# Bias terms of two mixture-of-experts layers: from fp32 matmuls to bfloat16 matmuls on three-part splits

## The chip, the cores and the metric

The kernel runs on one core of a Trainium2 chip. Its time is the device time of one execution in microseconds (us). The core's engines work in parallel, each through its own instruction stream in a fixed order: TensorE (PE, matmuls), VectorE (DVE), ScalarE (ACT), GpSimd (POOL, which here issues gathers and scatters by index) and SyncE (SP, which issues DMAs). They wait for each other through semaphores.

## What is computed

A network of four layers on 3125 nodes of width 256 (padded to 25 tiles of 128 rows) with 53125 edges. Each layer is a graph part and a dense part, each with a residual. The change concerns the dense parts of layers 2 and 3:

```python
# layer 2: eight experts, all used, weighted by a softmax router
w = softmax(feat @ Wr + br)
h = relu(bn(einsum('bfd,edh->bfeh', x, W1) + b1))
h = relu(bn(einsum('bfeh,ehk->bfek', h, W2) + b2))
y = einsum('bfeh,ehd->bfed', h, Wo) + bo            # bo: 8 x 256
out = einsum('bfed,fe->bfd', y, w)
# layer 3: a shared MLP and four experts, the two best gates per node
shared = relu(relu(x @ sW1 + sb1) @ sW2 + sb2) @ sW3 + sb3     # sb3: 1 x 256
o = einsum(relu(... experts ...), eW3) + eb3                   # eb3: 4 x 256
gates = softmax(x @ gW + gb); topv, topi = top_k(gates, 2)
out = shared + sum(softmax(topv) * o[topi])
```

In both layers the experts' last bias enters the output as (weights of the node) x (bias table): a product with a contraction of 8 or of 4.

## The kernel before

The program is laid out by a scheduler: it takes the operations as the code lists them, and fixes the order on each engine by its own estimates, so that a listed operation can move past others. The work goes through the layers in turn. The edges are worked on in 52 chunks of 8 tiles of 128 edges, the nodes in seven groups (GROUPS): six of four tiles and one of a single tile.

**Layer 2.** The edge loop is in l2_sorted (L1032 to L1089): for each chunk SP loads xw, row and rb (L1017 to L1024), TensorE makes the filters and messages, VectorE multiplies (xs, L1075), and POOL adds the rows into tables in memory (L1089). In its twelfth pair of tiles it calls late_weights, which loads all weights of the dense part: W1, W2, Wo (large), Wr, the router's bias br, bo (plain, one DMA), and two sets of normalisation vectors b, g, be, m, v, which VectorE folds together (L1130 to L1133). Then comes dense_sorted. For each group, choose (L1219 to L1232) makes the router's weights v (128 nodes x 8 per tile), transposes them on TensorE (L1230, one transpose per tile) and copies them to vT (8 x 128 per tile). experts then runs eight experts, two layers of fp32 matmuls into ph (L155) and ScalarE's ReLU to SBUF (L1249), and the last layer po, which VectorE adds with weight v into the residual (L1277). Ahead of the first expert's po, the bias term is one fp32 matmul per tile, vT against bo (L1269), 8 rows contracted, added at L1271. The choice for the next group is listed between the experts of the current one.

**Layer 3.** The edge loop is in l3_sorted: per chunk a load of the destination row (dl, L670), eight gathers of POOL (L208), masks sT (L679), maxima (ao L692, top L700, seg_m L431), products (L736) and a scatter as matmuls (L750). The first time a tile of nodes is met, its rows xh are loaded (L685). At its fifth chunk it calls l3_weights, which loads all weights of the dense part. A bias that is added by a matmul goes through bias3: load, split on VectorE into three bfloat16 parts (L1340, L1342) and a DMA that puts the parts on three rows (L1344); so it is for gb and sb3. eb3 is a plain load. sel is a 4 x 256 fp32 table of ones, made on POOL by blocks (L145 to L148), which spreads an expert's weight to the 64 rows of its hidden units. Then l3_dense: front, turn and choose make the gates of a group, spread transposes them (L852) and copies them to wT (L854), and experts runs the shared MLP and the experts. The expert's hidden values are multiplied by their gates at he (L894), with the gates spread by one fp32 matmul pk of sel and wT per pair of experts (L891, 4 rows contracted, 512 columns). The output po of a tile (L155) sums five matmuls: hs x sW3, ones x sb3 (bfloat16, 3 rows), wT x eb3 (fp32, 4 rows), and two of he x eW3. Each group's choice is listed inside the group before it (hooks 0 to 2).

What the change rewrites:

```python
                    self.mm(po, [(hs[:, c], w_["sW3"][:, 0, :]), (self.ones3, w_["sb3"]),
                                 (wT[:, j, :], w_["eb3"])]
                            + [(he[:, i, c], w_["eW3"][:, i, :]) for i in range(2)])
```

Of the kernel before, what the change touches and what calls it, by code (L numbers as in the profile page):

```python
# [8 lines left out]
F32 = mybir.dt.float32  # L9
BF = mybir.dt.bfloat16  # L10
# [7 lines left out]
P = 128  # L18
# [28 lines left out]
class Net:  # L47
# [93 lines left out]
    def blocks(self, pool, ne, width, name):  # L141

        nc = self.nc
        t = pool.tile([ne, ne * width], F32, name=name)
        nc.gpsimd.memset(t, 1.0)  # L145
        nc.gpsimd.affine_select(t, t, pattern=[[1, ne * width]], base=0, channel_multiplier=-width,
                                compare_op=ALU.is_ge, fill=0.0)
        nc.gpsimd.affine_select(t, t, pattern=[[-1, ne * width]], base=width - 1,  # L148
                                channel_multiplier=width, compare_op=ALU.is_ge, fill=0.0)
        return t  # L150


# [609 lines left out]
    def l3_weights(self, wp):  # L762
        w = {n: self.rows(wp, f"L3_ffn_{n}") for n in ("sW1", "sW2", "sW3", "eW1", "eW2", "eW3",
                                                       "gW")}
        w |= {n: self.plain(wp, f"L3_ffn_{n}") for n in ("sb1", "sb2", "eb1", "eb2")}
        w["gb"] = self.bias3(wp, "L3_ffn_gb")
        w["sb3"] = self.bias3(wp, "L3_ffn_sb3")
        w["eb3"] = self.plain(wp, "L3_ffn_eb3")
        w["sel"] = self.blocks(wp, 4, 64, "sel4")
        w["it"] = self.iota_row(wp, 4)  # L770
        return w

    def l3_dense(self, wp, o, a, b):

        nc, tc = self.nc, self.tc
        NE = 4
        w_ = self.l3w
        NG = len(GROUPS)
        with ExitStack() as ctx:
            work = ctx.enter_context(tc.tile_pool(name="work", bufs=2))  # L780
            psum = ctx.enter_context(tc.tile_pool(name="psum", bufs=2, space=PSUM))
            ab = work.tile([P, 2, D], F32, name="ab", bufs=1)
            for i, v in enumerate((a, b)):
                tp = psum.tile([P, 2, P], F32, name="tp")
# [3 lines left out]
            ys, xTs, ws = {}, {}, {}  # L788
# [57 lines left out]
            def spread(g):  # L846

                t0, n = GROUPS[g]
                oh = ws[g]
                tp = psum.tile([NE, 4, P], F32, name="sm", bufs=1)  # L850
                for j in range(n):
                    nc.tensor.transpose(tp[:, j, :], oh[:, j, :], self.ident)  # L852
                wT = work.tile([NE, 4, P], F32, name="wT")
                nc.scalar.copy(wT[:, :n], tp[:, :n])  # L854
                ws[g] = wT

            def experts(g, hooks):
                t0, n = GROUPS[g]
                w = n * P
                xT, wT = xTs.pop(g), ws.pop(g)  # L860

                def hidden(to, pairs, b):
                    ph = psum.tile([P, 4 * P], F32, name="ph", bufs=3)
                    self.mm(ph[:, :w], pairs)
                    nc.scalar.activation(to[:, :w], ph[:, :w], AF.Relu, bias=b)

                h1 = work.tile([P, 2, 4 * P], F32, name="h1")
                for f in range(2):
                    hidden(h1[:, f, :], [(w_["sW1"][:, k, f * P:(f + 1) * P], xT[:, k, :w])
                                         for k in range(2)], w_["sb1"][:, f:f + 1])  # L870
                hooks.get(0, lambda: None)()
                e1s = []
                for e in range(NE):
                    e1 = work.tile([P, 4 * P], F32, name="e1", bufs=5)
                    hidden(e1, [(w_["eW1"][:, 2 * e + k, :], xT[:, k, :w]) for k in range(2)],
                           w_["eb1"][:, e:e + 1])
                    e1s.append(e1)
                hooks.get(1, lambda: None)()
                hs = work.tile([P, 4 * P], F32, name="hs")
                hidden(hs, [(w_["sW2"][:, k, :], h1[:, k, :w]) for k in range(2)], w_["sb2"])  # L880
                he = work.tile([P, 2, 4 * P], F32, name="he")
                for i in range(2):
                    ph = psum.tile([P, 4 * P], F32, name="ph", bufs=3)
                    for j in range(2):
                        e = 2 * i + j
                        nc.tensor.matmul(ph[64 * j:64 * j + 64, :w], w_["eW2"][:, e, :],  # L886
                                         e1s[e][:, :w], start=True, stop=True)
                    r = work.tile([P, 4 * P], F32, name="r")
                    nc.scalar.activation(r[:, :w], ph[:, :w], AF.Relu, bias=w_["eb2"][:, i:i + 1])
                    pk = psum.tile([P, 4 * P], F32, name="ph", bufs=3)  # L890
                    nc.tensor.matmul(pk[:, :w], w_["sel"][:, i * P:(i + 1) * P],  # L891
                                     wT[:, :n].rearrange("e t p -> e (t p)"), start=True,
                                     stop=True)
                    nc.vector.tensor_mul(he[:, i, :w], r[:, :w], pk[:, :w])  # L894
                hooks.get(2, lambda: None)()
                y = work.tile([P, 4, D], F32, name="yo")
                for j in range(n):
                    t = t0 + j
                    c = slice(j * P, (j + 1) * P)
                    po = psum.tile([P, D], F32, name="po")  # L900
                    self.mm(po, [(hs[:, c], w_["sW3"][:, 0, :]), (self.ones3, w_["sb3"]),
                                 (wT[:, j, :], w_["eb3"])]
                            + [(he[:, i, c], w_["eW3"][:, i, :]) for i in range(2)])
                    nc.vector.tensor_add(y[:, j, :], self.x[:, t, :], po)
                    r = P if t < NT - 1 else LAST
                    nc.sync.dma_start(self.out[t * P:t * P + r, :], y[:r, j, :])
                hooks.get(3, lambda: None)()
# [208 lines left out]
    def late_weights(self, wt, after):  # L1116

        nc = self.nc
        self.after = after
        w1, w2, wo = (self.rows(wt, f"L2_ffn_{n}") for n in ("W1", "W2", "Wo"))  # L1120
        wr = self.rows(wt, "L2_ffn_Wr")
        br = self.bias3(wt, "L2_ffn_br")
        bo = self.plain(wt, "L2_ffn_bo")

        ab = []
        for i in "12":
            b_, g_, be, m_, v_ = (self.plain(wt, f"L2_ffn_{n}{i}")
                                  for n in ("b", "g", "be", "m", "v"))
            r = self.rsqrt(wt, v_, 1e-3, [P, 16], f"bn{i}")
            nc.vector.tensor_mul(r, r, g_)  # L1130
            nc.vector.tensor_sub(b_, b_, m_)
            nc.vector.tensor_mul(b_, b_, r)
            nc.vector.tensor_add(b_, b_, be)  # L1133
            ab.append((r, b_))
        w = self.with_attention(wt, "L3_gnn_W", 8, ("L3_gnn_att_src", "L3_gnn_att_dst"))
        self.after = None
        return w1, w2, wo, wr, br, bo, ab, w

    def dense_sorted(self, tables, wu1, bu1, wu2, bu2, gamma, beta, late):

        nc, tc = self.nc, self.tc
        w1, w2, wo, wr, br, bo, ab, w3 = late
        NE = 8
        with ExitStack() as ctx:
# [66 lines left out]
            def choose(g):  # L1211

                t0, n = GROUPS[g]
                xT = xTs[g] = turned(g, xTs[g])
                pl = psum.tile([P, 4, NE], F32, name="sm", bufs=1)
                for j in range(n):
                    self.mm(pl[:, j, :], [(xT[:, k, j * P:(j + 1) * P], wr[:, k, :])
                                          for k in range(2)] + [(self.ones3, br)])
                v = work.tile([P, 4, NE], F32, name="v")  # L1219
                mx = work.tile([P, 4], F32, name="mx")  # L1220
                mb = mx[:, :n].unsqueeze(2).to_broadcast([P, n, NE])
                nc.vector.tensor_reduce(mx[:, :n], pl[:, :n], axis=AX.X, op=ALU.max)
                nc.vector.tensor_sub(v[:, :n], pl[:, :n], mb)
                nc.scalar.activation(v[:, :n], v[:, :n], AF.Exp)
                nc.vector.tensor_reduce(mx[:, :n], v[:, :n], axis=AX.X, op=ALU.add)
                nc.vector.reciprocal(mx[:, :n], mx[:, :n])
                nc.vector.tensor_mul(v[:, :n], v[:, :n], mb)
                pT = psum.tile([NE, 4, P], F32, name="sm", bufs=1)
                for j in range(n):
                    nc.tensor.transpose(pT[:, j, :], v[:, j, :], self.ident)  # L1230
                vT = work.tile([NE, 4, P], F32, name="vT")
                nc.scalar.copy(vT[:, :n], pT[:, :n])  # L1232
                ws[g] = v, vT

            def experts(g, hooks):
                t0, n = GROUPS[g]
# [1024 lines left out]
```

## Time and profile before

| | us |
|---|---|
| median of 3 runs | 3889.32 |
| lowest and highest of them | 3887.5, 3907.43 |
| the profiled execution | 4120.86 |
| its span, first to last instruction | 4119.1 |
| layer 2: first to last bias matmul (L1269) | 2535.0 to 3086.2 |
| layer 3: first to last matmul with eb3 | 3935.8 to 4112.5 |

The profile is of one execution, with times from the start of its span. An instruction's line begins with its start and duration in us, then the engine, the line of the code, the operation, out<-in, the shape and how many in a row. An fp32 matmul is recorded as two. Matmuls overlap, so their durations add up to more than the time they take; their starts do not. "idle before" in brackets is how long the engine had stood still, and what released it. PEclk is the clock that TensorE was granted, in tenths of full speed in the page, as a fraction in a table of stretches. The tables by stretches give for each engine its busy time in that stretch with the number of instructions in brackets. Names lose their numbers in the trace: L_ffn_bo is layer 2's bo, and L_ffn_eb and L_ffn_sb in the matmuls of po are eb3 and sb3.

### The profile page before, as it was taken

How to read it: one execution, taken by the hardware profiler on the slowest of the kernel's cores; microseconds unless marked ns; L12 is line 12 of the kernel's file. 1: busy time of each engine (PE TensorE's matmuls, PEld its weight loads, DVE VectorE, ACT ScalarE, POOL GpSimd, SP SyncE). 2: the span in 40 equal slices, each digit the busy share in tenths (PEclk: the TensorE clock that was granted, in tenths of full speed). 3: DMA queues.
4: the chain of work that ended last, by engine and by line, in shares of the span. 5: the costliest groups of instructions: out<-in, count | busy, mean ns of one | idle time of the engine just before them, and what ended most of it. 6: DMA issues, size and time to landing. Idle time of an engine off the chain costs nothing. (4 is left out here: it accounts for less than half of the span.)

```text
span 4119.1 us, 46662 instructions
## 1 busy us (share of the span) xinstructions
PE 3364.1 (82%) x15552; PEld 2332.5 (57%) x15552; DVE 2200.9 (53%) x5404; ACT 966.1 (23%) x2102; POOL 1683.2 (41%) x1510
## 2 busy tenths in 40 slices
PE   3598879999996367999999989999992456665699
PEld 2365367777773245777777754556662344544554
DVE  4672379999998237433434333222332455655741
ACT  2222200000001124444444423333331000000142
POOL 4200146666661217777777740000005455654000
PEclk7799989999998679999999999999996677777789
DMA  4631378888882467887777860000004443443000
GB/s 129 201 125 44 134 230 270 284 281 272 272 274 71 146 202 195 165 133 128 134 132 128 134 136 3 6 6 6 6 6 126 113 111 104 117 111 100 21 11 22
DMA packets 339898, 524.03 MB, mean 127 GB/s; under 512 B 64375, under 2 KB 246849, under 8 KB 339649
## 3 DMA queue, kind: packets, MB, share of 16 engines
q0 software_dynamic: 125040, 236.91, 26.9%
q1 hardware_dynamic: 207217, 276.70, 21.3%
q10 hardware_dynamic: 7392, 7.34, 0.5%
q8 instruction: 126, 2.06, 0.2%
q14 instruction: 123, 1.01, 0.1%
HBM read 389.15 MB, written 131.64 MB: 126 GB/s over the span
## 5 line engine op out<-in xcount | busy, mean ns | idle before, releaser
L1089 POOL DMA_INDIRECT t<-sm,to x416 | 659.5, 1585 | 191.4 <-ACT sm L1086 68.4
L208 POOL DMA_INDIRECT kv<-kv_d,src_i x416 | 428.1, 1029 | 616.8 <-DVE s L412 348.3
L208 POOL DMA_INDIRECT xa<-xa_d,src_i x416 | 397.4, 955 | 312.6 <-issue 232.6
L155 PE MATMUL pe<-L_gnn_We,ea 128*128 128x256 f32 x1664 | 442.6, 389 | 28.9 <-issue 11.8
L750 PE MATMUL acc<-xa,s 128*128 128x272 f32 x1312 | 380.1, 445 | 89.1 <-DVE s L741 50.3
L155 PEld LDWEIGHTS <-sT 128*128 128x128 bf16 x3152 | 271.1, 100 | 279.8 <-issue 180.3
L1072 PE MATMUL pf<-L_gnn_Wf,hf 128*128 128x256 f32 x1664 | 419.7, 396 | 7.6 <-ACT hf L1035 7.6
L750 PEld LDWEIGHTS acc<-xa,s 128*128 128x128 f32 x1312 | 278.1, 219 | 166.8 <-DVE s L741 52.4
L1072 PEld LDWEIGHTS pf<-L_gnn_Wf,hf 128*128 128x128 f32 x1664 | 302.6, 192 | 88.9 <-issue 46.9
L1075 DVE TENSOR_TENSOR xs<-xs,pf 128x512 f32<-128x512 f32 x208 | 142.8, 687 | 376.9 <-PE pf L1072 338.3
L155 PEld LDWEIGHTS pe<-L_gnn_We,ea 128*128 128x128 f32 x1664 | 294.5, 194 | 85.2 <-DVE kv L526 31.7
L145 POOL MEMSET sel<- 4x256 f32 x1 | 0.3, 302 | 688.8 <-PE tp L155 688.8
L526 DVE TENSOR_TENSOR kv<-kv,pe 128x1024 f32<-128x1024 f32 x208 | 254.5, 1223 | 23.9 <-remote 19.4
L554 PE MATMUL acc<-kv,s 128*128 128x264 f32 x832 | 225.0, 395 | 11.1 <-DVE kv L549 6.9
L1084 PE MATMUL ps<-xs,m 128*128 128x256 f32 x832 | 217.0, 384 | 20.6 <-DVE xs L1075 16.3
L1249 ACT ACTIVATE h<-ph,L_ffn_b,bn_r 128x512 f32<-128x512 f32 (+1 forms) x224 | 162.8, 732 | 290.3 <-PE ph L155 289.9
L1277 DVE SCALAR_TENSOR_TENSOR xres<-po,v,xres 128x256 f32<-128x256 f32 x200 | 96.2, 482 | 247.7 <-PE po L155 247.4
L1086 ACT COPY sm<-ps 128x512 f32<-128x512 f32 x208 | 121.9, 586 | 451.3 <-PE ps L1084 363.3
L155 PE MATMUL po<-L_ffn_Wo,h 128*128 128x256 f32 x800 | 196.2, 389 | 0.0
L155 PE MATMUL qx<-qw,sT 128*128 128x256 bf16 x1248 | 190.9, 275 | 4.9 <-DVE pr L528 3.7
L155 PE MATMUL ph<-xT,L_ffn_W 128*128 128x512 f32 (+1 forms) x448 | 185.3, 553 | 0.5 <-ACT h L1249 0.5
L1084 PEld LDWEIGHTS ps<-xs,m 128*128 128x128 f32 x832 | 159.3, 192 | 44.5 <-issue 10.6
(434 smaller groups left out, 5424.1 us busy)
## 6 DMA issues: line engine op xcount, KB each, us to landing
ea<-in_edge_attr_dram SPq DMA_DIRECT2D x52, 1024.0 KB
dl<-dlT_d SPq DMA_DIRECT2D x156, 256.0 KB
row<-src_d SPq DMA_DIRECT2D x52, 512.0 KB
xs_d<-zero SPq DMA_DIRECT2D x2, 7168.0 KB
xg<-xs_d SPq DMA_DIRECT2D x28, 512.0 KB
t<-zero SPq DMA_DIRECT2D x4, 3328.0 KB
seg<-seg_d SPq DMA_DIRECT2D x52, 256.0 KB
qw<-q_d SPq DMA_DIRECT2D x52, 192.0 KB
```

The lines of the kernel that those rows point to most:

```text
L155: self.nc.tensor.matmul(out, l, r, start=(i == 0), stop=(i == len(pairs) - 1))
L208: self.nc.gpsimd.indirect_dma_start(out=out, out_offset=None, in_=table, in_offset=bass.IndirectOffsetOnAxis(ap=ids, axis=0))
L526: nc.vector.tensor_add(kvv, kvv, pe[:, :, None, :].to_broadcast([P, 2, 2, D]))
L554: nc.tensor.matmul(acc, s1[:, j, :], kv[:, j, D:], start=((t + j) % EL == 0), stop=((t + j) % EL == EL - 1))
L750: nc.tensor.matmul(accs[T][:, :R + 8], s1[:, i, :], xa[:, j, :], start=begins and i == 0, stop=last[T] == b and j == js[-1])
L1072: nc.tensor.matmul(pf[:, j, :], hf[:, c % 4, k, j * P:(j + 1) * P], wf2[:, k, :], start=False, stop=j + k == 2)
L1075: nc.vector.tensor_mul(xs, xs, pf)
L1084: nc.tensor.matmul(ps[:, j, :], m[:, (2 * c + j) % EL, :], xs[:, j, :], start=True, stop=True)
L1086: nc.scalar.copy(sm, ps)
L1089: nc.gpsimd.indirect_dma_start(out=tables[(2 * c + j) % len(tables)], in_=sm[:, j, :], in_offset=None, compute_op=ALU.add, out_offset=bass ...
L1249: nc.scalar.activation(h[:, f, :w], ph[:, :w], AF.Relu, scale=ab[i][0][:, c:c + 1], bias=ab[i][1][:, c:c + 1])
L1277: nc.vector.scalar_tensor_tensor(xv[:, i, :], po[:, i, :], v[:, j + i, e - 2:e - 1], xv[:, i, :], op0=ALU.mult, op1=ALU.add)
```

## The change

The weights of a node's experts and the bias tables are each split into three bfloat16 parts (value, remainder, remainder of that), and all nine products of parts are summed in one bfloat16 matmul: 9 x 8 = 72 rows in layer 2, 9 x 4 + 3 = 39 in layer 3, whose last three rows are ones against the parts of sb3. New functions, with the calls that use them:

```diff
+    def products(self, pool, names, ones):
+        nc = self.nc
+        k, n = self.ins[names].shape
+        t = pool.tile([9 * k + (3 if ones else 0), n], BF, name=f"{names}_9")
+        def parts(name, k):
+            a = pool.tile([8, n], F32, name="pr_a")[:k]
+            self.held(a)
+            nc.sync.dma_start(a, self.ins[name])
+            p = pool.tile([8, 3, n], BF, name="pr_p")[:k]
+            for i in range(3):
+                nc.vector.tensor_copy(p[:, i, :], a)
+                if i < 2:
+                    nc.vector.tensor_sub(a, a, p[:, i, :])
+            return p
+        p = parts(names, k)
+        for j in range(3):
+            for i in range(3):
+                r = (3 * j + i) * k
+                nc.sync.dma_start(t[r:r + k, :], p[:, j, :])
+        if ones:
+            nc.sync.dma_start(t[9 * k:, :], parts(ones, 1))
+        return t
+    def thirds(self, work, psum, v, n, k, ones):
+        nc = self.nc
+        w = 9 * k + (3 if ones else 0)
+        r = work.tile([P, 4, w], BF, name="w9")
+        if ones:
+            nc.vector.memset(r[:, :n, 9 * k:], 1.0)
+        d = work.tile([P, 4, k], F32, name="w9_d")
+        for i in range(3):
+            part = r[:, :n, i * k:(i + 1) * k]
+            nc.vector.tensor_copy(part, v if i == 0 else d[:, :n])
+            if i < 2:
+                nc.vector.tensor_sub(d[:, :n], v if i == 0 else d[:, :n], part)
+        for j in range(1, 3):
+            nc.vector.tensor_copy(r[:, :n, 3 * j * k:3 * (j + 1) * k], r[:, :n, :3 * k])
+        tp = psum.tile([w, 4, P], F32, name="sm", bufs=1)
+        for j in range(n):
+            nc.tensor.matmul(tp[:, j, :], r[:, j, :], self.identb, start=True, stop=True)
+        t = work.tile([w, 4, P], BF, name="wT")
+        nc.scalar.copy(t[:, :n], tp[:, :n])
         return t
...
-        w["sb3"] = self.bias3(wp, "L3_ffn_sb3")
-        w["eb3"] = self.plain(wp, "L3_ffn_eb3")
-        w["sel"] = self.blocks(wp, 4, 64, "sel4")
+        w["b3"] = self.products(wp, "L3_ffn_eb3", "L3_ffn_sb3")
+        sel = self.blocks(wp, 4, 64, "sel4")
+        b = wp.tile([4, 4 * 64], BF, name="sel4_b")
+        self.nc.vector.tensor_copy(b, sel)
+        w["sel"] = wp.tile([39, 4 * 64], BF, name="sel39")
+        self.nc.vector.memset(w["sel"], 0.0)
+        for i in range(3):
+            self.nc.sync.dma_start(w["sel"][4 * i:4 * i + 4, :], b)
...
-                oh = ws[g]
-                tp = psum.tile([NE, 4, P], F32, name="sm", bufs=1)
-                for j in range(n):
-                    nc.tensor.transpose(tp[:, j, :], oh[:, j, :], self.ident)
-                wT = work.tile([NE, 4, P], F32, name="wT")
-                nc.scalar.copy(wT[:, :n], tp[:, :n])
-                ws[g] = wT
+                ws[g] = self.thirds(work, psum, ws[g], n, NE, True)
...
-                    self.mm(po, [(hs[:, c], w_["sW3"][:, 0, :]), (self.ones3, w_["sb3"]),
-                                 (wT[:, j, :], w_["eb3"])]
+                    self.mm(po, [(hs[:, c], w_["sW3"][:, 0, :]), (wT[:, j, :], w_["b3"])]
...
-        bo = self.plain(wt, "L2_ffn_bo")
+        bo = self.products(wt, "L2_ffn_bo", None)
...
-                pT = psum.tile([NE, 4, P], F32, name="sm", bufs=1)
-                for j in range(n):
-                    nc.tensor.transpose(pT[:, j, :], v[:, j, :], self.ident)
-                vT = work.tile([NE, 4, P], F32, name="vT")
-                nc.scalar.copy(vT[:, :n], pT[:, :n])
-                ws[g] = v, vT
+                ws[g] = v, self.thirds(work, psum, v[:, :n], n, NE, False)
```

The matmuls L891 and L1269 are written as before; their operands are now bfloat16 tiles of 39 and 72 rows. In order of engines: SP issues 21 DMAs more (nine for bo, nine for eb3, three for sel39), and between the loads of late_weights and l3_weights; VectorE gets the splits of the tables (five operations each), a cast and a memset for sel39, and seven (layer 2) or eight (layer 3) small operations per group; ScalarE's copy of the transposed weights writes bfloat16 and more rows.

More of the change, by code (lines that the diff above doesn't have):

```diff
@@ L149, in blocks @@
                                 channel_multiplier=width, compare_op=ALU.is_ge, fill=0.0)
+        return t
[20 more added lines that the diff above has]
+            nc.sync.dma_start(t[9 * k:, :], parts(ones, 1))
+        return t
+    def thirds(self, work, psum, v, n, k, ones):
[17 more added lines that the diff above has]
+        nc.scalar.copy(t[:, :n], tp[:, :n])
         return t
```

## The prediction

> **What bounds the kernel now.** I read the page first (shares, then the 40 slices), then the stretches of the span that the change touches, then the order of time on single engines inside them.
>
> ```profile
> PE 3364.1 (82%) x15552; PEld 2332.5 (57%) x15552; DVE 2200.9 (53%) x5404; ACT 966.1 (23%) x2102; POOL 1683.2 (41%) x1510
> ...
> PE   3598879999996367999999989999992456665699
> ...
> PEclk7799989999998679999999999999996677777789
> ```
>
> TensorE is busiest, but only in some slices. A saved matmul is worth its time only where the PE row shows 9, so I cut the span by stage:
>
> ```profile
> core 0: us, PE busy (x) PEld busy (x) DVE busy (x) ACT busy (x) POOL busy (x), PEclk, DMA share, GB/s
> ...
> 1600.00:1680.00 80.00, 68.42 (x360) 48.70 (x358) 51.23 (x184) 42.09 (x103) 55.70 (x35) 0.94 0.99 235
> 1680.00:2430.00 750.00, 740.85 (x4189) 554.30 (x4188) 291.06 (x1082) 302.19 (x546) 585.32 (x371) 1.00 0.78 127
> ...
> 2600.00:3095.00 495.00, 494.49 (x1734) 299.77 (x1733) 152.72 (x451) 172.12 (x270) 0.00 (x0) 0.99 0.02 6
> 3115.00:3250.00 135.00, 26.87 (x173) 19.77 (x173) 38.05 (x93) 5.54 (x18) 77.54 (x85) 0.55 0.52 145
> 3250.00:3910.00 660.00, 401.63 (x1958) 309.30 (x1957) 381.73 (x853) 51.81 (x193) 321.08 (x336) 0.76 0.35 95
> 3910.00:3930.00 20.00, 12.55 (x61) 9.87 (x61) 17.59 (x68) 12.06 (x27) 0.00 (x0) 0.67 0.00 1
> 3930.00:4119.00 189.00, 183.90 (x646) 96.76 (x646) 55.25 (x240) 57.35 (x99) 0.00 (x0) 0.93 0.05 18
> ```
>
> The fourth row is layer 2's dense experts and the last is layer 3's: TensorE fills 99.9% and 97% of them, VectorE 31% and 29%. There matmul time is kernel time. The rows 1600 to 1680 and 3115 to 3250 are where the weights are loaded. The first is crowded in its DMA (0.99), the second in nothing: layer 3's edge loop waits for latencies.
>
> **What it removes on TensorE.** The durations of single matmuls overlap, so I take start to start:
>
> ```profile
> 2626.57 1.13 PE L1269 MATMUL po<-L_ffn_bo,vT 8*128 8x256 f32 x4
> 2627.63 1.13 PE L155 MATMUL po<-L_ffn_Wo,h 128*128 128x256 f32 x4
> ...
> 4017.68 1.12 PE L891 MATMUL ph<-wT,sel 4*128 4x512 f32 x2
> 4018.73 1.08 PE L886 MATMUL ph<-e,L_ffn_eW 128*64 128x512 f32 x4
> ...
> 4020.79 0.60 PE L852 MATMUL sm<-ident,oh 128*4 128x128 f32 x4
> 4021.22 0.60 PE L155 MATMUL po<-L_ffn_sW,hs 128*128 128x256 f32 x2
> 4021.75 0.28 PE L155 MATMUL po<-L_ffn_sb,ones 3*128 3x256 bf16 x1
> 4021.87 0.59 PE L155 MATMUL po<-L_ffn_eb,wT 4*128 4x256 f32 x2
> 4022.40 0.92 PE L155 MATMUL po<-L_ffn_eW,he 128*128 128x256 f32 x3
> ```
>
> An fp32 matmul shows as two records. L1269: 4 records, two matmuls, 1.06 us, 0.53 each. L891: 1.05. The transposes of L852 (an identity matmul of one record each): 0.43 for four, 0.11 each. The bf16 matmul of sb3, 256 wide: 0.12. The expert bias after it: 0.53.
>
> Layer 2: 25 tiles x (0.53 - 0.12) = 10.3 us. The transposes become bf16 matmuls with 128 columns to stream, half of sb3's; I take half of its 0.12, so they save 25 x 0.05 = 1.3. Together 11.5 us.
>
> Layer 3, each group of four tiles: po loses the separate bias matmul and turns the fp32 one to bf16, (0.12 + 0.53) - 0.12 = 0.53 a tile, 2.1 us; transposes 0.2; L891 twice. For a bf16 matmul 512 wide the nearest row is layer 2's loop:
>
> ```profile
> 1700.94 0.38 PE L1068 MATMUL pf<-L_gnn_bf,ones 3*128 3x512 bf16 x1
> 1701.26 1.99 PE L1072 MATMUL pf<-L_gnn_Wf,hf 128*128 128x256 f32 x8
> ```
>
> That is 0.32 us. [...] So a full group saves 1.46 + 2.1 + 0.2 = 3.8 us, six of them 22.7; the one-tile group about 1.0. Together 23.7 us at full clock, a little more in the profiled execution, whose clock was 0.93 there. That 36 or 39 or 72 rows are contracted instead of 4 or 8 costs nothing by these rows: 3 rows took 0.12, and xe's 128 rows took 0.13 (1700.18 to 1700.94 for six).
>
> **What it adds on VectorE and ScalarE in these stages.** Per group seven small operations in layer 2 and eight in layer 3, about 0.2 us each and 0.21 start to start, so 1.5 to 1.7 us between the weights and their transposes. Layer 2: the weights were ready at 2693.7 (L1227 at 2693.51, 0.19 long), so the parts are at 2695.2, or 2695.7 with one L1277 of 0.48 between. The changed order puts the transposes behind two more ph matmuls, which end near 2696: a stall of 0 to 0.3 us a group, I take 1 us in all. ScalarE's copy stays as large (0.57). Layer 3: choose ends at 4043.6, the transposes come at 4051.2; 7.6 us of cover for 1.7, so nothing. Without that cover it would be 6 x 1.7 = 10 us. Only the first, one-tile group has none: VectorE fills 17.6 of 20 us there, so 8 operations at 0.15 to 0.21 cost about 2 us. The he products wait for L891's result as before, but it comes sooner; VectorE stays far below full, so TensorE remains the bound.
>
> **What it adds in loading.** Layer 2's bias goes through VectorE (five operations of 8x256, 0.3 to 0.4 each, 1.7 us) and nine scattering DMAs, inserted on SP between these and the loop's own loads:
>
> ```profile
> 1640.12 0.33 SPq L129 DMA_DIRECT2D L_ffn_v<-in_L_ffn_v_dram  x1
> 1640.54 0.38 SPq L129 DMA_DIRECT2D L_ffn_b<-in_L_ffn_b_dram  x1
> 1641.01 0.39 SPq L129 DMA_DIRECT2D L_ffn_g<-in_L_ffn_g_dram  x1
> ...
> 1645.28 0.38 SPq L1020 DMA_DIRECT2D xw<-x_d  x1
> ```
>
> SP issues one each 0.45 us: 9 x 0.45 = 4 us, by which m, v, w_att and the next chunks' xw, row and rb move back. PE waited 4.5 us for that xw (at 1650.41) already. From 1680 TensorE is full (741 of 750), so lateness is not made up: +4 us, bounds 0 (gather and scatter waits cover it) and 8 (the nine also wait for the split on VectorE, with xs multiplications, L1075, queued behind). [...]
>
> Layer 3's weights: twelve more DMAs on SP (nine parts, three for sel39; sb3's one takes the place of its old one), and on VectorE five small operations more for eb3, a cast and a memset. SP already hangs here:
>
> ```profile
> 3147.45 0.47 SPq L685 DMA_DIRECT2D xh<-xa_d  x1
> 3176.45 0.76 SPq L1344 DMA_DIRECT2D L_ffn_gb<-L_ffn_gb_p  x1
> ```
>
> It waits 28.5 us for the split of gb, which stands on VectorE behind a 26.12 us wait at L692. Before, dl of two further chunks was issued ahead of this block; in the changed order only one is, and the other comes after nine scatters, gb's, a seg load and the load of sb3, 12 x 0.45 = 5 us after the block lifts. Who waits: sT (L679), then pa, then the ao and top of that chunk; and VectorE's split of sb3 waits for the nine DMAs, since it reuses their tile. Below nothing: earlier order could also help this latency-bound stretch. Bounds -10 to +50; I take +3, since VectorE reaches those chunks only at 3185 to 3188, about when the late load lands. The cast of sel waits for POOL's blocks, done at 3118.5: nothing.
>
> **Sum.** -11.5 + 1 (layer 2), -23.7 + 2 (layer 3), +4 and +3 (loads) = -25 us. In the profiled execution: 4120.86 (span 4119.1) to about 4096. That execution stands 231 us above the median of 3889.32, mostly in layer 3's loop and clock, which the change's gains don't touch; the dense stages ran near full clock, so I carry the 25 us over unscaled: 3864 us, -0.65%. About 0.5%, 19 us, is what this measurement can tell from no change.
>
> **Rivals.**
> 1. Layer 3's loop start gets worse (slower). Place: SP's block at 3147 to 3176 and the POOL stall that follows:
>
> ```profile
> 3239.80 0.95 POOL L208 DMA_INDIRECT xa<-xa_d,src_i  x1 [26.98 <-DVE top L700]
> ```
>
> POOL runs nine chunks ahead and then stands until top of a chunk is done. If the late dl holds that chunk up for one more round of each of the two long waits (26 and 27 us), it costs 53 us: -25 - 3 + 53 = +25, 3914. It decides from 47 us of loss on (-28 + 47 = +19). Against it: a late dl of 5 us needs to fall exactly ahead of each wait.
> [...]
> 3. The chain takes TensorE's place in the dense stages (same): each layer 3 group stalls the 1.7 us of its parts, and layer 2's 1.5 (6 x 1.7 + 6 x 1.5 = 19 in place of 1, net -7): 3882. Against: 7.6 us of cover.
> [...]
>
> **Chances.** My sum 0.50 (3855 to 3869, nearly all of it faster); more 0.11; rivals 2 and 3 together 0.26; slower 0.13. Range: 3848 to 3902, down to the full gain, up past the "same" cases into the middle of a partial rival 1.
>
> **What would show it.** Stretch lengths: layer 2's dense stage (first to last bias matmul, 2535.0 to 3086.2) shorter by about 10 us; layer 3's period per group (28.7 us, 4051.18 to 4079.87) shorter by 3.8; PE still over 97% in both; w9 copies with no idle time of PE after them; layer 2's loop ending 4 us later; layer 3's loop (3115 to 3910) unchanged within 10. Wrong if PE idles before the transposes, or if the loop of layer 3 has moved by tens of us in either direction.

## The result and the profile after

The changed kernel takes 3860.23 us (median of 6 runs, 3853.04 to 3862.93), the kernel before 3893.38 beside it (6 runs, 3886.88 to 3907.43). The ratio is 0.9898, 95% interval 0.9878 to 0.9919: about 1% faster, 33 us by the medians. The forecast was faster by 25 us, and the time lies inside its range. The profiled execution took 3854.27 us, its span 3852.5. One run of the changed kernel in a later set took 5951.81 us at a mean clock of 0.56, a slow state, and is left out of what follows.

For comparing stages the first profile of before is not the best partner: it was taken where layer 3's gathers take longer (the last 344 of the 416 in 588 us; in nine other profiles of this study in 432 to 434, in the three of the last set, all of one chip, again in 577 to 603). A second profile of before (3896.18 us, span 3894.5) stands beside the changed one here. All lengths run from the first or last instruction named to the next, in us. An "output" of layer 3 is VectorE's addition of a finished tile po to the residual (L904 before, 25 in all):

| stage, ending with | before, second profile | changed | forecast of the difference |
|---|---|---|---|
| layer 2's edge loop: first filter matmul to last store matmul | 892.0 | 895.1 | +4 |
| layer 2's dense stage: first ph to last Wo matmul | 596.1 | 580.0 | -10.5 |
| layer 3's edge loop: first gather to last scatter matmul | 564.4 | 564.5 | +3 |
| start of layer 3's dense stage: to the first output | 48.8 | 49.5 | +2 |
| layer 3's dense stage: first to last output | 183.0 | 150.2 | -23.7 |

The two dense stages in the changed kernel, as stretches:

```profile
core 0: us, PE busy (x) PEld busy (x) DVE busy (x) ACT busy (x) POOL busy (x), PEclk, DMA share, GB/s
...
2512.00:3047.00 535.00, 535.00 (x1874) 323.38 (x1872) 172.86 (x530) 185.71 (x283) 0.00 (x0) 1.00 0.02 6
3694.00:3846.00 152.00, 152.00 (x553) 80.75 (x551) 58.65 (x267) 54.34 (x97) 0.00 (x0) 0.97 0.06 20
```

TensorE has no idle time in either, so the small VectorE work did not make it wait. The matmuls themselves, in order of time:

```profile
2692.38 0.38 PE L1312 MATMUL po<-L_ffn_bo,wT 72*128 72x256 bf16 x2
2692.60 1.03 PE L205 MATMUL po<-L_ffn_Wo,h 128*128 128x256 f32 x4
...
3765.62 0.39 PE L940 MATMUL ph<-wT,sel 39*128 39x512 bf16 x1
3765.93 1.08 PE L935 MATMUL ph<-e,L_ffn_eW 128*64 128x512 f32 x4
...
3767.26 0.40 PE L197 MATMUL sm<-identb,w 128*39 128x128 bf16 x4
3767.59 0.70 PE L205 MATMUL po<-L_ffn_sW,hs 128*128 128x256 f32 x2
...
3796.60 0.59 PE L205 MATMUL po<-L_ffn_sW,hs 128*128 128x256 f32 x2
3797.12 0.28 PE L205 MATMUL po<-L_ffn_eb,wT 39*128 39x256 bf16 x1
3797.33 1.13 PE L205 MATMUL po<-L_ffn_eW,he 128*128 128x256 f32 x4
3798.30 0.59 PE L205 MATMUL po<-L_ffn_sW,hs 128*128 128x256 f32 x2
```

From start to start, two bias matmuls of layer 2 now take 0.22 (1.06 before), L891 (now L940) 0.31 (1.05), four transposes 0.33 (0.43). Layer 3's bias matmul takes 0.21, not 0.12. It is not the fp32 matmul behind it that makes the difference: layer 2's second bias matmul stands ahead of an fp32 one too and takes 0.11. What differs is the number of rows contracted: 72 ahead of 128 there, 39 ahead of 128 here. A tile of po, from one sW3 matmul to the next, takes 1.70 us. In the kernel before, the same tile in the second profile:

```profile
3852.42 0.59 PE L155 MATMUL po<-L_ffn_sW,hs 128*128 128x256 f32 x2
3852.95 0.28 PE L155 MATMUL po<-L_ffn_sb,ones 3*128 3x256 bf16 x1
3853.07 0.59 PE L155 MATMUL po<-L_ffn_eb,wT 4*128 4x256 f32 x2
3853.59 1.13 PE L155 MATMUL po<-L_ffn_eW,he 128*128 128x256 f32 x4
3854.56 0.59 PE L155 MATMUL po<-L_ffn_sW,hs 128*128 128x256 f32 x2
```

That is 2.14 us, so a tile saves 0.44, not 0.53. The 0.12 of sb3's bfloat16 matmul, from which the forecast was made, is three rows ahead of four. The same matmul ahead of an eb3 matmul that is padded with zeros to 128 rows (the kernel pad_eb3 below) takes 0.21:

```profile
4071.15 0.28 PE L162 MATMUL po<-L_ffn_sb,ones 3*128 3x256 bf16 x1
4071.36 0.70 PE L162 MATMUL po<-L_ffn_eb,wT 128*128 128x256 f32 x2
```

In fp32 it is the same: the last record of eb3 stands 0.30 us ahead of he x eW3 with four rows, 0.22 with 128. So in these traces the step from few rows to 128 costs about 0.1 us, whatever the type. Why 72 rows go without it, no run shows, and no run gives layer 3's table more rows.

A full group of layer 3 at full clock went from 28.69 us (L891 to L891) to 25.49. Six groups at 3.2 are 19 us. The stage gave 32.8. Most of the rest is in the granted clock, which the experiments below take up.

### The profile page after: what moved, and what is told of

The parts are those of the page before. It is cut to its first block, busy times and chain, and to the rows that moved or that the text cites. A ratio compares the mean times of both kernels' runs of the same rounds, so it can differ in the third digit from the quotient of the medians.

```text
span 3852.5 us, 46616 instructions
## 1 busy us (share of the span) xinstructions
PE 3275.6 (85%) x15463; PEld 2288.4 (59%) x15463; DVE 2219.3 (58%) x5521; ACT 964.6 (25%) x2102; POOL 1682.6 (44%) x1510
## 5 line engine op out<-in xcount | busy, mean ns | idle before, releaser
L800 PE MATMUL acc<-xa,s 128*128 128x272 f32 x1312 | 348.6, 423 | 77.6 <-DVE s L791 77.6
L800 PEld LDWEIGHTS acc<-xa,s 128*128 128x128 f32 x1312 | 263.5, 207 | 138.4 <-DVE s L791 80.8
L1132 PE MATMUL ps<-xs,m 128*128 128x256 f32 x832 | 217.0, 384 | 16.8 <-DVE xs L1123 12.4
L205 PE MATMUL xe<-xw,sT 128*128 128x256 bf16 x1248 | 173.1, 276 | 14.7 <-DMA xw<-x_d 10.0
```

The lines of the kernel that those rows point to most:

```text
L205: self.nc.tensor.matmul(out, l, r, start=(i == 0), stop=(i == len(pairs) - 1))
L800: nc.tensor.matmul(accs[T][:, :R + 8], s1[:, i, :], xa[:, j, :], start=begins and i == 0, stop=last[T] == b and j == js[-1])
L1132: nc.tensor.matmul(ps[:, j, :], m[:, (2 * c + j) % EL, :], xs[:, j, :], start=True, stop=True)
```

## The experiments

"Time lost to half clock" in what follows is worked out from the clock record: of a stage, half of the time in which the clock record stands at 0.5; of a run, its span x (1 - mean granted clock). At 0.5 a tile of po took 4.03 us (first profile of before, from 3987.98), at full clock 2.13 (from 3998.95). Where TensorE also stands idle, as in layer 3's edge loop (401.63 of 660 us busy from 3250 to 3910 in that profile), this is an upper estimate.

**The kernel before, a second profile.** No edit.

> The kernel before once more, unchanged, for a second profile: the first one's span was 4119 us, about 230 above the median, and 181 us of the difference to the changed kernel's profile lay in layer 3's gathers (705 against 524 us from first to last). Theory (the gain lies in the two dense stages): a span near 3890, layer 3's gathers 520 to 530 us, layer 2's dense stage (first to last Wo matmul) 574 us as in the first profile, layer 3's from the last scatter matmul to the last output about 222. Rival (part of the gain came from layer 3's loop, reordered by the new loads): gathers over 535 us.

Measured: span 3894.5, layer 3's gathers 524 us (first to last), layer 3's edge loop 564.4, against 564.5 in the changed kernel. The loop gave nothing, so the rival falls. Layer 3's dense stage is 183.0 us here and was 174.0 in the first profile, though its matmuls are the same: 16.8 us lost to half clock here, 6.8 there, 2.0 in the changed kernel.

**Each layer alone.** Layer 2's part alone keeps of the change the lines of late_weights and choose; layer 3's part alone keeps the others.

```diff
-        w["b3"] = self.products(wp, "L3_ffn_eb3", "L3_ffn_sb3")
+        w["sb3"] = self.bias3(wp, "L3_ffn_sb3")
+        w["eb3"] = self.plain(wp, "L3_ffn_eb3")
...
```

> Layer 2's part alone (bo through products, thirds in choose), layer 3 as before. Theory: the dense stage of layer 2 gives about 16 us (574.2 against 559.2 from first to last Wo matmul in the two profiles) and its loads cost about 2.5 (first to last store matmul of the loop 865.7 against 868.2): 13 us faster, ratio 0.9965. [...]

> Layer 3's part alone (products, sel39, thirds in spread), layer 2 as before. Theory: the dense stage gives 22 to 24 us and the loads at the start of the edge loop cost 0 to 4: about 20 faster, ratio 0.995. Rival (SP's longer block at the loop's start holds up a chunk): under 12 us, ratio above 0.997, with the loop over 5 us longer than in the kernel before.

Measured: layer 3 alone 3868.2 us against 3892.37, ratio 0.994 (0.9923 to 0.9958), as expected. Layer 2 alone 3891.79, ratio 0.9999 (0.9987 to 1.0012): no gain, although its dense stage took 580.2 us as in the changed kernel and its loop 896.9. Its runs had a mean clock of 0.9141, those of before 0.9164; that is 334 against 325 us lost, 9 us. In its profile layer 1's dense part, ahead of anything that the change touches and with the same instructions, lost 83.6 us to half clock, against 66.0 in the second profile of before; but layer 3 alone, which did gain, lost 83.3 there in its profile, so one profile does not settle it. Taking each run's loss off its time leaves, on average, 3567.6 for before, 3558.4 for layer 2 alone, 3548.6 for layer 3 alone, 3540.5 for the changed kernel: -9.2 and -19.0 add up to -28.2, and the whole is -27.1. So the work adds up in these sets, and the clock moves on top of it.

**Layer 2 alone, once more.** No edit.

> Layer 2's part alone once more: its first measurement gave no gain (0.9999) although its stages add up to 11 us less, and its granted clock was 0.9141 on average against 0.9164. Theory (the clock of the stages ahead of the change varies by itself from one set of runs to the next): ratio 0.996 to 0.998 this time, with a mean clock like that of before. Rival (something in this kernel lowers the clock each time): 0.9999 again with 0.914.

Measured: 3894.17 us against 3902.37, ratio 0.9979 (0.9967 to 0.9992): the two sets give 0 and 8 us for a part whose stages say 11. Its mean clock was 0.9141 again, and before's in this set 0.9139. The ratio is the theory's, the clock of 0.914 is the rival's: it was before's clock that differed between the two sets, which ran on different chips. Why, no run shows.

**The loads alone.** The changed kernel's loads, with the matmuls and transposes of before on stand-in tables.

```diff
-                    self.mm(po, [(hs[:, c], w_["sW3"][:, 0, :]), (wT[:, j, :], w_["b3"])]
+                    self.mm(po, [(hs[:, c], w_["sW3"][:, 0, :]), (self.ones3, w_["b3"][:3, :]),
+                                 (wT[:, j, :], w_["sel"])]
...
-        bo = self.products(wt, "L2_ffn_bo", None)
+        self.products(wt, "L2_ffn_bo", None)
+        bo = self.pr
```

> All of the changed kernel's loads, splits and scatters, with the fp32 matmuls and transposes of before. It leaves out the bias tables' values: L1269 multiplies by what the split leaves over of bo, the eb3 matmul by sel and the sb3 matmul by parts of eb3, so shapes and types of every matmul are those of before and no load is added for them. Theory: 2 to 6 us slower than before, ratio 1.0005 to 1.0015, since issues on SP do not wait for each other's end. [...]

Measured: 3902.26 against 3892.37, ratio 1.0027 (1.0015 to 1.0039), 10 us by the medians, above the theory's 2 to 6. Layer 2's loop took 896.4 (+4.4), layer 3's 564.2; the other 6 are clock again (332 us lost against 325): 3570.7 against 3567.6 with the loss taken off, +3. The loads cost 3 to 5 us, in layer 2's loop, where SP shows them in the changed kernel:

```profile
1611.35 0.33 SPq L129 DMA_DIRECT2D L_ffn_v<-in_L_ffn_v_dram  x1
1612.07 2.20 SPq L174 DMA_DIRECT2D L_ffn_bo<-pr_p  x3
1614.38 0.72 SPq L1387 DMA_DIRECT2D L_ffn_br<-L_ffn_br_p  x1
...
1615.65 4.09 SPq L174 DMA_DIRECT2D L_ffn_bo<-pr_p  x6
...
1623.25 0.86 SPq L1068 DMA_DIRECT2D xw<-x_d  x2
```

Nine scatters take 6.3 us of SP, 0.7 each. I had taken 0.45 from loads out of memory; the row of the same kind, bias3's own scatter between tiles (L1344), had 0.66 to 0.86 in the first profile. The next chunk's xw is issued 11.9 us after v instead of 5.2, and the loop pays 3 to 5 of the 6.7. SP issues a DMA before an earlier one has landed: in the same profile it issued the load of br at 1603.66 and five more from 1604.04 to 1606.45, while VectorE waited for that of br until 1610.41 (7.59 us idle). When the scatters land, the trace does not show.

**The bias table earlier.** Layer 2's split and scatter at the start of layer 1's dense part.

```diff
+        with tc.tile_pool(name="prt", bufs=1) as tmp:
+            self.bo9 = self.products(wp, "L2_ffn_bo", None, tmp)
...
-        bo = self.products(wt, "L2_ffn_bo", None)
+        bo = self.bo9
```

> The changed kernel with layer 2's bias table split and scattered at the start of layer 1's dense part, ahead of layer 2's loop, instead of between the loop's loads. Theory (these issues cost the loop 3 to 4 us): the loop from the first filter matmul to the last store matmul 892 us as before instead of 895 to 897, about 3 us faster than the changed kernel, ratio 0.989. Rival (they cost as much wherever they are): the stage ahead of the loop longer by as much.

Measured: 3853.23 us against 3902.37, ratio 0.9882 (0.9861 to 0.9902). The loop took 889.0 us instead of 895.1, the stage ahead of it 245.9 against 244.3 to 244.5. Its median is the lowest of the study, but that it beats the changed kernel is not shown: the intervals overlap, and with the time lost to half clock taken off run by run the two are level (3541.1 and 3540.5). What speaks for it is the loop's 6 us, against 1.5 ahead of it, in one profile each, at equal loss in the loop (21 us). Why the loop is even shorter than in the kernel before (892.0, of which 24 lost), no run shows.

**The small operations of VectorE twice.**

```diff
-        for i in range(3):
+        for i in [0, 1, 2] * 2:
...
-        for j in range(1, 3):
+        for j in [1, 2] * 2:
```

> The changed kernel with the small VectorE operations of thirds issued twice over (the splits and the copies of both layers; the same values again), 7 more in a group, about 1.5 us. Theory (layer 3's chain lies under 7.6 us of cover, layer 2's just meets the transposes): layer 3's stage the same within 1 us but for the first group (1 to 2 us), layer 2's stage longer by 0 to 1.5 us a group, at most 9: ratio to before 0.990 to 0.992. Rival (the chain is on the path in both): 19 us over the changed kernel, ratio 0.995.

Measured: 3859.54 us, ratio 0.9895 (0.9874 to 0.9916), the changed kernel's. Layer 2's dense stage 580.7 (580.0), layer 3's outputs 152.4 with 4.1 lost to half clock, so 148.3 (148.2); to the first output 51.9 (49.5). Only the first group, without cover, pays, 2.4 us. In layer 2 the scheduler also set the transposes one ph matmul (two records) later, so there the cover is partly its doing.

**The old matmuls over 128 rows.** The kernel before, fp32 throughout; the short operands get zeros below.

```diff
-                wT = work.tile([NE, 4, P], F32, name="wT")
-                nc.scalar.copy(wT[:, :n], tp[:, :n])
+                wT = work.tile([P, 4, P], F32, name="wT")
+                nc.gpsimd.memset(wT, 0.0)
+                nc.scalar.copy(wT[:NE, :n], tp[:, :n])
...
-        bo = self.plain(wt, "L2_ffn_bo")
+        bo = self.padded(wt, "L2_ffn_bo")
```

> The kernel before, with the bias matmuls (L1269, the eb3 one) and the spreading matmul (L891) still in fp32 and as wide as before, but contracted over 128 rows, of which all but 8 or 4 are zero. In layer 3's dense stage the kernel before lost 16.8 us to half clock in its second profile and the changed one 2.0; in layer 2's 7.8 against 4.4. Theory (matmuls of few rows in fp32 let the granted clock fall, so that part of the gain is clock and not matmul time): half clock costs under 5 us in layer 3's stage and 4 to 5 in layer 2's, the last 25 outputs span 165 to 172 us instead of 183, ratio about 0.996. Rival (the clock's falls are where they happen to fall, whatever is contracted): 10 to 17 and 7.8 us as before, 183 us, ratio 1.000.

Measured: 3875.24 us against 3902.37, ratio 0.9935 (0.9917 to 0.9953), 0.65% faster with not one fp32 matmul fewer. The outputs span 169.9 us, 3.4 of them lost; 166.5 without the loss, 166.2 in the second profile of before. The mean clock of its runs was 0.9202, of before beside them 0.9139; with the loss taken off the two are 3566.7 and 3565.4. So padding changes the clock and not the work. The theory holds for layer 3. Layer 2's stage (592.4, 6.6 lost against 7.8) moved less, and missed the 4 to 5 expected. The two stages account for 17 us of the 27; the rest is clock elsewhere, which no profile of before on that chip places. Layer 3's dense stage in three stretches, before (second profile), then padded, then changed; the granted clock is the last column but two. The line ahead of before's three is a part of its first stretch, in which the clock fell:

```profile
3726.60:3736.70 10.10, 10.10 (x26) 6.00 (x25) 3.36 (x21) 1.29 (x3) 0.00 (x0) 0.50 0.08 28
3707.00:3869.80 162.80, 162.80 (x565) 83.45 (x563) 48.65 (x213) 53.99 (x94) 0.00 (x0) 0.95 0.05 17
3869.80:3873.30 3.50, 3.50 (x12) 1.08 (x10) 0.88 (x2) 1.38 (x2) 0.00 (x0) 1.00 0.01 2
3873.30:3890.00 16.70, 15.80 (x36) 8.82 (x34) 2.18 (x5) 0.00 (x0) 0.00 (x0) 0.50 0.08 26
```

```profile
3698.00:3855.50 157.50, 157.50 (x567) 84.71 (x565) 48.94 (x215) 54.01 (x94) 2.10 (x4) 0.98 0.05 18
3855.50:3859.00 3.50, 3.50 (x12) 1.13 (x10) 0.94 (x2) 1.37 (x2) 0.00 (x0) 1.00 0.01 2
3859.00:3868.00 9.00, 8.18 (x35) 5.73 (x34) 2.13 (x5) 0.00 (x0) 0.00 (x0) 1.00 0.17 50
```

```profile
3698.00:3838.60 140.60, 140.60 (x515) 74.31 (x513) 52.42 (x252) 49.61 (x90) 0.00 (x0) 0.99 0.06 20
3838.60:3842.00 3.40, 3.40 (x15) 1.59 (x14) 1.37 (x2) 1.37 (x2) 0.00 (x0) 1.00 0.01 2
3842.00:3848.20 6.20, 5.35 (x23) 3.31 (x21) 1.68 (x4) 0.00 (x0) 0.00 (x0) 1.00 0.20 67
```

The middle one of the three is the last group's two L891 and the eW2 matmuls beside them. TensorE has no idle time in it. Where L891 contracts four rows, the clock stands at 0.50 from its end on and the last outputs take 16.7 us; where it contracts 128 or is short, the clock stays and they take 9.0 or 6.2. All 13 profiles agree: in the six whose L891 contracts four rows in fp32, the clock stands at half for one stretch of 10 us or more inside the outputs (20.5 in one), and in four of them at the end as well; in the seven where L891 is padded or short, no stretch there exceeds 6.8 us and none is at the end. Single stretches of 3.4 us remain in the padded kernels; what causes those, no run shows.

**Which of layer 3's two.** Padding for L891 alone, and for the eb3 matmul alone.

```diff
-        w["eb3"] = self.padded(wp, "L3_ffn_eb3")
+        w["eb3"] = self.plain(wp, "L3_ffn_eb3")
...
-                                 (wT[:, j, :], w_["eb3"])]
+                                 (wT[:NE, j, :], w_["eb3"])]
```

> The kernel before with layer 3's spreading matmul (L891) alone contracted over 128 rows of which all but four are zero; eb3 and layer 2's bias matmul as before. With all three padded, layer 3's stage lost 3.4 us to half clock instead of 10 to 23 and the outputs spanned 169.9 us. Theory A (the four pk halves of 0.5 us are what lets the clock fall, being most of a 3.4 us stretch): 3 to 5 us lost, 170 us, ratio 0.994. Theory B (the bias matmuls in po count as much): 7 to 12 us lost, 174 to 178 us, ratio 0.997.

> The kernel before with the eb3 matmul alone contracted over 128 rows of which all but four are zero; L891 and layer 2's bias matmul as before. Theory A (pk lets the clock fall): 10 us or more lost to half clock in layer 3's stage, 176 to 189 us, ratio 0.998 to 1.000. Theory B (eb3 counts as much): 7 to 12 us lost, 174 to 178 us, ratio 0.997.

Measured, where the gathers are slow again and before takes 4132.68 us: L891 alone 4108.45, ratio 0.9932 (0.9911 to 0.9953), outputs 170.6 us with 3.7 lost, as theory A has it for this kernel. The eb3 matmul alone 4111.54, ratio 0.9942 (0.992 to 0.9964), outputs 173.9 with 6.8 lost. That ratio is far better than theory A gave it (0.998 to 1.000) and better than B (0.997), but its profile still has the stretch of 10.2 us and the 6.8 lost of the first profile of before. Both kernels also clear wT to zero on POOL, which therefore does not explain why only one of them lost the stretch. So padding L891 is enough to take the long stretches away; where the eb3 kernel's runs gain is not settled.

**The changed kernel once more.** No edit.

> The changed kernel once more, beside these. If what its first measurement showed holds: ratio 0.988 to 0.992, a mean clock of 0.917 to 0.918, layer 3's outputs within 149 to 153 us with under 4 us lost to half clock, layer 2's dense stage 580 us. If the first profile was lucky with the clock: 155 us or more with 8 us lost.

Measured beside these, by five runs: 4105.07 against 4132.68, ratio 0.9917 (0.9894 to 0.994). Layer 3's outputs 150.1 us with 2.0 lost, layer 2's dense stage 580.2: the lengths of the dense stages repeat to 0.2 us. The mean clock was 0.8928 (0.8903 before), short of the 0.917 expected, with the slow gathers. With the loss taken off run by run the gain in this set is 17 us (3663.9 against 3681.2), not the 27 of the first. In its profile 212 of the 440 us lost lie in layer 3's edge loop, where TensorE is not the bound, so the reckoning is rough here.

## Why the prediction was right, and by which sizes it was off

**Layer 2's dense stage, -11.5.** Right in mechanism; the measured difference is -16.1. By starts over the whole stage the bias matmuls went from 13.9 to 3.9 us (-10.0, forecast -10.3), the transposes from 2.7 to 1.4 (-1.3, as forecast). The stall of 1 us that I took was none: doubling the chain cost 0.7. What I didn't have: the time lost to half clock fell from 7.8 to 4.4, 3.4 us (7.6 to 7.8 in all six profiles with the eight-row bias matmul, 4.4 to 4.7 in all six with the new one). The last 1.4 are the Wo matmuls behind the bias matmuls: from the first to the second stood 0.34 us on average before (0.32 at full clock) and 0.22 after, and there are twelve such places. That is the step from eight rows to 128 again. (The row of 2600 to 3095 us, which the prediction calls the fourth, is the third of those it shows.)

**Layer 3's dense stage, -23.7.** The term that was too large is the po tile: 0.12 for the bfloat16 bias matmul was read where a four-row matmul followed; with a matmul over 128 rows behind it, it is 0.21, so 25 x 0.09 = 2.3 us less. The remark that 36, 39 or 72 rows cost nothing against 4 or 8 looked at the matmul's own rows alone; what counted here is the step to those of the next one (0.12 us with 3 rows ahead of 4, 0.21 ahead of 128). The transposes save 0.1 a group, not 0.2 (0.6 us), and the one-tile group's 1.0 falls ahead of the first output. L891 at 0.31 (0.32 from layer 2's row) was right. Without the loss the stage went from 166.2 to 148.2, -18.0; against the first profile of before it is -19.0. The last 1 to 2 us of the miss have no place. What was missing is the clock: 16.8 lost down to 2.0 in these two profiles, 6.8 down to 2.0 against the first. I had written that the excess of the first profile lay partly in the clock, "which the change's gains don't touch". That step failed: in layer 3 the old L891 goes with the long falls of the clock, and the change took them away.

**The start of layer 3's dense stage, +2.** It was 0.7, in which the one-tile group's saving is contained.

**Layer 2's loads, +4.** 3.1 in the changed kernel's profile, 4 to 5 in the kernels with the same loads; the scatter costs 0.7 us of SP, not 0.45, and the loop does not pay all of it.

**Layer 3's loads, +3.** 0.1, though SP issued the next dl only at 3124.99, behind eb3's scatters from 3117.21 on: the loop did not wait for it.

**The rivals.** Rival 1 is thereby out, and 3 by the doubled operations: forecast to cost 19 us, they cost 2.4 ahead of the first output and 0.8 in the two stages. Nor did rival 2 and "more" of the chances come: the loads cost 3.1 and 0.1 us, L891 takes 0.31, and 3860.23 lies within the 3855 to 3869 of the sum.

**The sum.** -16.1 + 3.1 + 0.1 + 0.7 - 32.8 = -45 between the two profiles (their spans differ by 42); the medians say -33, since the changed kernel's profiled run is 6 us below the median of its runs and the second profile of before 3 to 4 above. Without the loss the stages give -12.7 - 18.0 + 3.1 + 0.1 + 0.7 = -27, and the runs of the first sets say -27 as well, where 25 was forecast. That closeness is in part luck: layer 3's dense part was forecast 4 us too large, layer 2's 2 too small, and the loads 4 too dear. What the medians have beyond it, about 6 us, is clock, which the forecast put at nothing.

## What to carry to other kernels

Price an operation on TensorE start to start, in a place whose neighbours contract as many rows as its future neighbours will. A bfloat16 matmul 256 wide cost 0.21 us with 39 or 3 rows ahead of one with 128, 0.12 with 3 rows ahead of 4, and 0.11 with 72 rows ahead of 128.

In a stage where TensorE is the bound, look at the granted clock of that stage in more than one profile before you say that it stays: long matmuls with few rows may cost more than their own time, and padding them with zeros to 128 rows is a short test of that (here 3902.37 to 3875.24 us).

Times that differ by 10 us in 3900 can be clock alone (the kernel before had 3892.37 us at a mean clock of 0.9164 in one set, 3902.37 at 0.9139 in another), so compare run by run with the clock beside the time.

## What the hardware did that I had not expected

The granted clock of TensorE fell to half while TensorE was fully busy. In layer 3's dense stage of before (second profile), with 182.1 of 183.0 us busy, the clock record stands at half for stretches of 10.2, 3.4, 3.4 and 23.2 us, the last of them beyond the last output to the end of the span. In the 7 us ahead of each stretch TensorE had no idle time at all. The long stretches went with the number of rows that L891 contracts: 4 in the six profiles that have a stretch of 10 us or more inside the outputs, 128 (zeros in 124 of them) or 39 in the seven without, at nearly equal times of the matmuls (166.2 and 166.5 us for 4 and 128 rows, the loss taken off). How the number of rows bears on the clock, no run shows. The amount differs from one execution to the next: the kernel before lost 6.8 us in layer 3's outputs in one profile and 16.8 in the other, layer 2 alone 16.6 and 22.8; the new matmuls lost 0.9 to 4.1 in five profiles.
